# A selective scan's last D product moved over B's PSUM tile, and Gabor groups taken in pairs

## The chip, the cores and the metric

The kernel runs on one core of one Trainium2 chip. The metric is the device time of one execution in microseconds. A core has five engines that run side by side, each through its own instructions in order: TensorE (PE, matrix products, weight loads listed apart as PEld), VectorE (DVE), ScalarE (ACT), GpSimd (POOL) and SyncE (SP, which here only issues DMAs). They wait for each other by semaphores.

## The reference

The input is 4 images of 64 channels and 128x128 pixels. Four layers follow each other:

```python
# layer 0: Mamba block, 16 states, over all 65,536 pixels as one sequence
# layer 1: Gabor transform, two small block-diagonal products, softshrink, inverse
# layer 2: two 3x3 convolutions with batch norm, a channel gate, residual
# layer 3: two 3x3 convolutions; LayerNorm; Mamba block, 64 states, per image;
#          LayerNorm; feed-forward with a 3x3 depthwise convolution
def step(h, t):                      # the scan of both Mamba blocks, 128 inner channels
    h = h * exp(delta_t * A) + (delta_t * x_t) * B_t
    y_t = h @ C_t                    # y = ys + x * D;  y = y * silu(z)
```

In layer 1 each image is seen as a 128x128 grid with 64 channels. `R1`, an FFT over 32x32 blocks, two products with w1 and w2, a softshrink, an FFT back and a last product with the window give `I`, which is added to the image.

## The kernel before

**The scan (`_Mamba.run`, used by layers 0 and 3).** Time is cut into chunks of 1,024 pixels, 64 chunks a layer. Four of the states by 32 of the 128 channels fill the 128 partitions, so a *group* of four states takes four *steps* (j = 0 to 3, one for each quarter of the channels). Layer 0 has 4 groups a chunk, layer 3 has 16. A step has four parts:

- ACT computes `da` = exp(A·delta) into one of four buffers (L562);
- the input `bx` = delta·x·B is put into PSUM (below);
- DVE scans over the 1,024 columns (L599), from `da` and `bx`, into one of eight slots of `ring`;
- POOL multiplies the slot by C (L602), and PE later adds the states up into `y` (L419), which has one PSUM tile. The sums of a group are issued in the second and third step after its last; the first thing put into a chunk's `y` is x·D (L416), in the last step of its first group.

Groups come in two kinds, in a fixed order: "DADA" in layer 0, "DADAADAADADAADAA" in layer 3. In an *A* group ACT multiplies delta·x with B in transposed form (`bxT`, L393, 28 small instructions a group, and one block on POOL, L397), and PE transposes it into a PSUM tile for each step (L500, 8 transposes). In a *D* group PE spreads B over the partitions into one PSUM tile (L506), once for the group, and DVE multiplies it with a replicated copy of delta·x (`du`, one tile for each j, loaded by SP's DMAs) into a second PSUM tile (L593), for each step again into the same one.

PSUM has room for two `bx` tiles, which are taken in turn. So the transposes of the first A step after a D group take B's tile, and have to wait for the last product, which reads B.

The instructions of a step are written out in one order and each engine keeps it (`_Pin`): in step i come the `da` three steps ahead, bxT copies at a pace worked out from what is owed, the transposes for step i+1 (`produced(i + 1)`), the product of a D step, the scan, POOL's product, at most one entry of the list `owed` (y's first sums and the groups' sums), and at last pieces of the next and the last chunk's remaining work (`beside`): projections, convolution, normalisation, delta, all through one further PSUM tile `pm`. In layer 3 `budget` says how many pieces a step may issue: 2, 2, 2, 1 in the steps of a D group, none in A. In layer 0 it is 12 everywhere. The gating product `yg` = y·silu(z) (L625) is a DVE instruction in the last step of a chunk's first group, ahead of that step's product.

**The Gabor stage (`layer1`).** For each of 4 images and each of 4 groups of 16 channels PE runs a chain: fa (L1047, the image's columns, 16 products of 256 columns, copied by DVE to `Z`), fb (L1058, copied by ACT to `O`), w1 (L1071), w2 (L1078; DVE adds the bias and clamps, POOL subtracts the clamp: the softshrink, L1079 to L1082), ga (L1089, copied by ACT to `V`) and lt (L1100: for each of 32 rows two products of 64 columns, which DVE adds to the image, L1107). All six share four PSUM tiles. Each group waits for the one before it.

Of the kernel before, what the change touches and what calls it, by code (L numbers as in the profile page):

```python
# [10 lines left out]
F32 = mybir.dt.float32  # L11
AF = mybir.ActivationFunctionType
ALU = mybir.AluOpType
# [4 lines left out]
P = 128  # L18
B, C, HH, WW = 4, 64, 128, 128
HW = HH * WW  # L20
TC = 1024
NH = TC // 512
DI = 128
NUM, SIZE = 4, 32
NQ, DD = 4, 32
ND = DI // DD
# [5 lines left out]
G = 16  # L32
# [135 lines left out]
class _Mamba:  # L168
# [19 lines left out]
    def __init__(self, ctx, tc, K, nst, w, kinds, bufs, slots={}):  # L188
# [5 lines left out]
        self.dram = ctx.enter_context(tc.tile_pool(name="md", bufs=2, space=DRAM))  # L194
        self.bp = ctx.enter_context(tc.tile_pool(name="mb", bufs=1, space=PSUM))
        self.misc = ctx.enter_context(tc.tile_pool(name="mm", bufs=1, space=PSUM))

# [229 lines left out]
    def run(self, chunks, ahead, behind, leads, budget):  # L427
# [23 lines left out]
        reps = [(k, c, j) for c in chunks for k in ("dl", "du") for j in range(ND)]  # L451
        das, bxs = {}, {}
        nexp = nmul = nC = 0
# [37 lines left out]
        def produced(i):  # L491

            if i == n:
                return
            v, j = its[i]
            if v["kind"] == "A" or i == v["at"]:
                bx = bxs[i] = self.bp.tile([P, TC], F32, name="bx", tag="bx", bufs=2)
            if v["kind"] == "A":
                for k in range(NB):
                    nc.tensor.transpose(  # L500
                        bx[:, P * k : P * (k + 1)], v["bxT"][:, k, :, :, j].rearrange("p q e -> p (q e)"), self.K.eye
                    )
            elif i == v["at"]:
                v["B"] = bx
                for k in _COLS:
                    nc.tensor.matmul(bx[:, k], self.spread[v["g"]], v["c"]["xc"][:, k], start=True, stop=True)  # L506
# [25 lines left out]
        at = -1  # L532
# [5 lines left out]
        for i, (u, j) in enumerate(its):  # L538
# [46 lines left out]
            if full and full[0] <= i:  # L585
                started(behind(full[1], self.gated(full[1])), i)
                full = None
            produced(i + 1)
            if u["kind"] == "D":
                if i == u["at"]:  # L590
                    u["bx"] = self.bp.tile([P, TC], F32, name="bx", tag="bx", bufs=2)
                bxs[i] = u["bx"]
                nc.vector.tensor_mul(bxs[i], u["c"]["du"][j], u["B"])  # L593

# [4 lines left out]
            nc.vector.tensor_tensor_scan(  # L599
                hs, das.pop(i), bxs.pop(i), 0.0 if u["c"].get("reset") else st, ALU.mult, ALU.add  # L600
            )
            nc.gpsimd.tensor_mul(hc, hs, u["cb"])  # L602
            if j == ND - 1:
                nc.gpsimd.tensor_copy(self.state[:, :, u["g"]], self.ring[:, slot - j : slot + 1, GAP + TC - 1])
            u["hc"].append(hc)
            if i == u["last"]:
                owed += [(i, u, None)] * (u["g"] == 0) + [(i + 2, u, h) for h in range(NH)]
            while owed and not full and (owed[0][0] <= i or i + 1 == n):
# [362 lines left out]
def layer1(ctx, tc, K, w, x1, x2):  # L971
# [60 lines left out]
    MU = P // G  # L1032
    for b in range(B):
        X = xp.tile([P, HH, C], F32, name="X1", tag="X1")
        nc.sync.dma_start(X, x1[b].rearrange("c (h r w) -> (c h) r w", h=2, w=C))
        for g in range(NG):
            ch = slice(g * G, (g + 1) * G)

            def ps():
                return pa.tile([P, 1024], F32, name="p1", tag="p1")  # L1040


            Z = wp.tile([P, 2, P, G], F32, name="Z", tag="Z", bufs=2)
            for c0 in range(0, G, 4):
                p = ps().rearrange("p (c i m) -> p c i m", c=4, i=2)
                for c in range(4):
                    nc.tensor.matmul(  # L1047
                        p[:, c], X[:, :, g * G + c0 + c], fa.rearrange("p i m k -> p (i m k)"), start=True, stop=True
                    )
                nc.vector.tensor_copy(Z[:, :, :, c0 : c0 + 4].rearrange("p i m c -> p c i m"), p)  # L1050

# [22 lines left out]
            for k0 in range(0, G, 8):  # L1074
# [6 lines left out]
                nc.vector.tensor_scalar(cl, xs[:, ks], -LAMBD, LAMBD, ALU.max, ALU.min)  # L1081
                nc.gpsimd.tensor_sub(xs[:, ks], xs[:, ks], cl)  # L1082

            V = wp.tile([P, 2, G, P], F32, name="V", tag="V", bufs=2)
            xr = xs.rearrange("p k (m c) -> p (k m) c", c=G)
            for c0 in range(0, G, 4):
                p = ps().rearrange("p (c i m) -> p c i m", c=4, i=2)
                for c in range(4):
                    nc.tensor.matmul(  # L1089
                        p[:, c], xr[:, :, c0 + c], ga.rearrange("p i m k -> p (i m k)"), start=True, stop=True  # L1090
                    )
                nc.scalar.copy(V[:, :, c0 : c0 + 4, :].rearrange("p i c m -> p c i m"), p)

            Vl = V.rearrange("p i c (y l) -> p i l y c", l=SIZE)
            Xl = X[:, :, ch].rearrange("p (y l) c -> p l y c", l=SIZE)
            for l0 in range(0, SIZE, 16):
                p = ps().rearrange("p (l y c) -> p l y c", l=16, y=NUM)
                for l in range(16):
                    for i in range(2):
# [6 lines left out]
                        )  # L1106
                nc.vector.tensor_add(Xl[:, l0 : l0 + 16], Xl[:, l0 : l0 + 16], p)  # L1107
        nc.sync.dma_start(x2[b].rearrange("c (h r w) -> (c h) r w", h=2, w=C), X)
# [175 lines left out]
def layer3_mamba(ctx, tc, K, w, t3, x3, s3, n3):  # L1284
# [78 lines left out]
    chunks = [{"at": (b, t0), "reset": t0 == 0} for b in range(B) for t0 in range(0, HW, TC)]  # L1363
    m.run(chunks, ahead, behind, (64, 36), [x for k in m.kinds for x in ([2, 2, 2, 1] if k == "D" else [0] * ND)])

# [280 lines left out]
```

## Time and profile before

| what | value |
|---|---|
| median of 3 runs (lowest, highest) | 19,391.08 us (19,358.28, 19,392.66) |
| the profiled execution | 19,395.58 us, span 19,393.5 us |
| mean granted PE clock | 0.876 |
| DVE busy | 15,837.4 us (82%) |
| PE busy | 15,226.3 us (79%) |
| ACT busy | 14,924.4 us (77%) |
| POOL busy | 14,204.5 us (73%) |
| first and last scan of layer 0 | 68.3 and 3,663.0 us |
| first and last scan of layer 3 | 6,229.6 and 18,427.1 us |

In a line of the profile stand the line of the kernel, the engine, the operation, the tiles (written <- read), the shape and the count; then busy time, the mean of one in ns, the engine's idle time just before such instructions, and who ended it. A line of a timeline has the start, the length, the engine, the line, the operation and the count of equal instructions merged into it; idle time before it and its releaser stand in brackets. Lengths of neighbours can overlap. A matmul in fp32 shows as two records, a transpose as one.

### The profile page before, as it was taken

The page shows a single profiled execution, that of the slowest core. Times are in us where ns is not written, and L with a number is a line of the kernel's source. Part 1 is how long each engine was busy: PE and PEld are TensorE (multiplying, and loading weights), DVE is VectorE, ACT ScalarE, POOL GpSimd, SP SyncE. Part 2 cuts the span into 40 slices and gives each one's busy share as a digit, 9 for nine tenths or more (in the row PEclk, how much of TensorE's full clock was granted, in tenths as well). Part 3 has the DMA queues.
Part 4 walks back from the last instruction along what each step waited for, and adds up shares of the span by engine and source line. Part 5 has one row for each costly group of instructions (what it writes and reads, how often), then busy time and mean ns, then how long its engine had stood idle before and what let it go on. Part 6 is the DMA issues. An engine that isn't in the chain of part 4 may idle for free. (4 is left out here: it accounts for less than half of the span.)

```text
span 19393.5 us, 238514 instructions
## 1 busy us (share of the span) xinstructions
PE 15226.3 (79%) x80186; PEld 7611.8 (39%) x80186; DVE 15837.4 (82%) x8739; ACT 14924.4 (77%) x30369; POOL 14204.5 (73%) x8094
## 2 busy tenths in 40 slices
PE   7777878778797777777777777777777777777799
PEld 3333333367434333333333333333333333333323
DVE  7888888722113999999999999999999999999977
ACT  7888888501223898989889988989898988888833
POOL 6888888600001989898989989998989989898900
PEclk8989889879898888888888888888888888888899
DMA  5555555300122323232323233232323232323222
GB/s 140 148 156 150 151 154 150 116 38 27 34 69 74 84 78 87 75 88 76 87 76 86 80 83 83 79 87 76 88 76 87 76 86 78 84 80 82 73 56 55
DMA packets 669522, 1722.88 MB, mean 89 GB/s; under 512 B 196784, under 2 KB 231936, under 8 KB 660864
## 3 DMA queue, kind: packets, MB, share of 16 engines
q1 hardware_dynamic: 668288, 1707.62, 32.5%
q8 instruction: 629, 10.31, 0.2%
q14 instruction: 605, 4.96, 0.1%
HBM read 1434.27 MB, written 272.63 MB: 88 GB/s over the span
## 5 line engine op out<-in xcount | busy, mean ns | idle before, releaser
L602 POOL TENSOR_TENSOR ring<-ring,cb 128x1024 f32<-128x1024 f32 x5120 | 12081.8, 2376 | 1642.8 <-DVE ring L599 1335.9
L599 DVE TENSOR_TENSOR_SCAN ring<-da,state,bx 128x1024 f32<-128x1024 f32 x4848 | 11144.0, 2336 | 962.5 <-PE bx L500 687.9
L562 ACT ACTIVATE da<-dl,A 128x1024 f32<-128x1024 f32 x5120 | 5868.1, 1146 | 1370.1 <-DVE ring L599 1353.7
L393 ACT ACTIVATE bxT<-duT,BT 128x128 f32<-128x128 f32 x21504 | 6757.3, 387 | 0.0
L500 PE MATMUL bx<-cst,bxT 128*128 128x128 f32 x24576 | 4455.8, 338 | 2837.7 <-DVE bx L593 2045.6
L500 PEld LDWEIGHTS bx<-cst,bxT 128*128 128x128 f32 x24576 | 3740.9, 214 | 4905.5 <-DVE bx L593 2064.0
L419 PE MATMUL y<-ring,cst 128*32 128x512 f32 x20480 | 3560.4, 658 | 335.2 <-POOL ring L602 334.7
L593 DVE TENSOR_TENSOR bx<-du,bx 128x1024 f32<-128x1024 f32 x2048 | 2515.1, 1228 | 338.1 <-PE bx L506 217.5
L419 PEld LDWEIGHTS y<-ring,cst 128*32 128x32 f32 x20480 | 531.5, 112 | 1741.5 <-POOL ring L602 864.5
L1151 PE MATMUL cv<-img,cw 64*64 64x512 f32 x9216 | 1008.9, 594 | 76.3 <-DMA img<-d_x 45.5
L506 PE MATMUL bx<-xc,spread 128*128 128x512 f32 x2048 | 1016.9, 619 | 1.4
L1082 POOL TENSOR_TENSOR xs<-xs,cl 128x1024 f32<-128x1024 f32 x32 | 74.9, 2340 | 1066.7 <-DVE cl L1081 1066.7
L1316 POOL MEMSET X<- 64x1 f32 x4 | 0.4, 91 | 1125.1 <-DMA cw<-in_l_conv_wT 1125.1
L397 POOL TENSOR_TENSOR bxT<-duT,BT 128x512 f32<-128x512 f32 x768 | 809.0, 1053 | 11.9 <-ACT duT L376 11.9
L1151 PEld LDWEIGHTS cv<-img,cw 64*64 64x64 f32 x9216 | 435.8, 134 | 647.3 <-issue 534.8
L599 DVE TENSOR_TENSOR_SCAN ring<-da,bx 128x1024 f32<-128x1024 f32 x272 | 609.2, 2276 | 71.1 <-PE bx L500 49.4
L1447 ACT ACTIVATE h<-ph,ff_fc_b 128x384 f32<-128x384 f32 (+1 forms) x384 | 200.8, 577 | 594.2 <-PE ph L1442 576.5
L1433 POOL MEMSET h<- 128x18 f32 x64 | 8.3, 131 | 876.1 <-PE pd L1521 443.9
L1521 PE MATMUL pd<-h,diag 64*64 64x512 f32 x4608 | 632.1, 603 | 0.7 <-issue 0.7
L506 PEld LDWEIGHTS bx<-xc,spread 128*128 128x128 f32 x2048 | 347.6, 189 | 687.4 <-issue 463.6
L1467 DVE SCALAR_TENSOR_TENSOR g<-h,dww,g 128x2048 f32<-128x2048 f32 x256 | 602.0, 2351 | 11.4 <-DVE g L1467 0.5
L1065 ACT COPY O<-p 128x1024 f32<-128x1024 f32 x32 | 32.4, 1012 | 690.9 <-PE p L1058 690.9
(321 smaller groups left out, 13274.4 us busy)
## 6 DMA issues: line engine op xcount, KB each, us to landing
cb<-c SPq DMA_DIRECT2D x5120, 128.0 KB, 2.9
dl<-d SPq DMA_DIRECT2D x2048, 128.0 KB, 3.5
du<-d SPq DMA_DIRECT2D x2048, 128.0 KB, 3.1
d<-pos SPq DMA_DIRECT2D x128, 512.0 KB, 2.6
d<-u SPq DMA_DIRECT2D x128, 512.0 KB, 3.0
X<-d_t SPq DMA_DIRECT2D x124, 256.0 KB, 4.1
S<-in_x SPq DMA_DIRECT2D x120, 256.5 KB, 4.5
res<-in_x SPq DMA_DIRECT2D x128, 128.0 KB, 3.8
```

Of the source, the lines that this page charges most:

```text
L393: nc.scalar.activation(t[:, k, q].rearrange("p e j -> p (e j)"), c["duT"][:, k, :], AF.Copy, scale=c["BT"][:, k, n : n + 1])
L397: nc.gpsimd.tensor_mul(t[:, k].rearrange("p q e j -> p q (e j)"), c["duT"][:, k].unsqueeze(1).to_broadcast(shape), c["BT"][:, k, NQ * g : ...
L419: nc.tensor.matmul(c["y"][DD * j : DD * (j + 1), _COLS[h]], K.sel, hc[:, _COLS[h]], start=False, stop=u["g"] == self.ng - 1,)
L500: nc.tensor.transpose(bx[:, P * k : P * (k + 1)], v["bxT"][:, k, :, :, j].rearrange("p q e -> p (q e)"), self.K.eye)
L506: nc.tensor.matmul(bx[:, k], self.spread[v["g"]], v["c"]["xc"][:, k], start=True, stop=True)
L562: nc.scalar.activation(das[nexp], v["c"]["dl"][k], AF.Exp, scale=self.A[:, k, v["g"] : v["g"] + 1])
L593: nc.vector.tensor_mul(bxs[i], u["c"]["du"][j], u["B"])
L599: nc.vector.tensor_tensor_scan(hs, das.pop(i), bxs.pop(i), 0.0 if u["c"].get("reset") else st, ALU.mult, ALU.add)
L602: nc.gpsimd.tensor_mul(hc, hs, u["cb"])
L1151: nc.tensor.matmul(p[i][half[h]], W[half[i], k, :], src[half[i], at : at + 4, dx : dx + WW], start=k == 0, stop=k == 8,)
L1467: nc.vector.scalar_tensor_tensor(g1, tap, wk, g1, ALU.mult, ALU.add)
L1521: nc.tensor.matmul(pd[i][half[h]], diag[half[i], k, :], h0[half[i], r : r + 4, dx : dx + WW], start=k == 0, stop=k == 8,)
```

## The change

1. The two `bx` tiles are made once and addressed by number. B of a D group and the products of its steps 0, 1 and 2 stand as before, in two tiles. The product of step 3 is written over B, in place.
2. That product is issued in step 2, right behind step 2's own product, ahead of the scan of step 2. So DVE's order in a D group is product, scan, product, scan, product, product, scan, scan. The first A step after it takes the tile of the products, not B's.
3. Layer 3's budget in the last step of a D group is 0 instead of 1. In each chunk this moves one piece of the output projection from step 11 to step 20, and one piece of the next chunk's B from step 43 to step 52.
4. The entry of x·D in `owed` is made in the first step of the group instead of the last, with the same due step.
5. In the Gabor stage fa of the next group is issued ahead of ga of the present one, and lt runs once for two groups: 64 products of 128 columns instead of 128 of 64. `V` holds two groups, in one buffer instead of two. DVE's additions keep their number and size.

```diff
+        self.bx = [self.bp.tile([P, TC], F32, name=f"bx{k}") for k in range(2)]
...
-            if v["kind"] == "A" or i == v["at"]:
-                bx = bxs[i] = self.bp.tile([P, TC], F32, name="bx", tag="bx", bufs=2)
             if v["kind"] == "A":
+                at = tiles[i] = 1 - tiles.get(i - 1, 1)
+                bx = self.bx[at]
...
             elif i == v["at"]:
-                v["B"] = bx
+                at = 1 - tiles.get(i - 1, 1)
+                tiles.update({i + k: at if k == ND - 1 else 1 - at for k in range(ND)})
+                bx = v["B"] = self.bx[at]
...
+            bx = self.bx[tiles[i]]
             if u["kind"] == "D":
-                if i == u["at"]:
-                    u["bx"] = self.bp.tile([P, TC], F32, name="bx", tag="bx", bufs=2)
-                bxs[i] = u["bx"]
-                nc.vector.tensor_mul(bxs[i], u["c"]["du"][j], u["B"])
+                for k in {ND - 2: (ND - 2, ND - 1), ND - 1: ()}.get(j, (j,)):
+                    nc.vector.tensor_mul(self.bx[tiles[i - j + k]], u["c"]["du"][k], u["B"])
...
+            if i == u["at"] and u["g"] == 0:
+                owed.append((u["last"], u, None))
             if i == u["last"]:
-                owed += [(i, u, None)] * (u["g"] == 0) + [(i + 2, u, h) for h in range(NH)]
+                owed += [(i + 2, u, h) for h in range(NH)]
...
-    ... ([2, 2, 2, 1] if k == "D" else [0] * ND)])      # layer 3's budget
+    ... ([2, 2, 2, 0] if k == "D" else [0] * ND)])
...
+    def transformed(b, g):          # fa and Z, as before; loads the image where g is 0
+    Zn = transformed(0, 0)
     for b in range(B):
         for g in range(NG):
+            Z = Zn                  # then fb, w1, w2 and the softshrink, as before
...
-            V = wp.tile([P, 2, G, P], F32, name="V", tag="V", bufs=2)
+            if (b, g) != (B - 1, NG - 1):
+                Zn = transformed(*divmod(b * NG + g + 1, NG))
+            if g % 2 == 0:
+                V = wp.tile([P, 2, 2 * G, P], F32, name="V", tag="V")
+            v0 = g % 2 * G          # ga, copied to V[:, :, v0 + c0 : v0 + c0 + 4]
+            if g % 2 == 0:
+                continue
...
-            Xl = X[:, :, ch].rearrange("p (y l) c -> p l y c", l=SIZE)
-            for l0 in range(0, SIZE, 16):
-                p = ps().rearrange("p (l y c) -> p l y c", l=16, y=NUM)
-                for l in range(16):
+            Xl = X[:, :, (g - 1) * G : (g + 1) * G].rearrange("p (y l) c -> p l y c", l=SIZE)
+            for l0 in range(0, SIZE, 8):
+                p = ps().rearrange("p (l y c) -> p l y c", l=8, y=NUM)
+                for l in range(8):
```

## The prediction

> **What bounds the kernel now.** I read the busy times by stage first, then the page's costliest groups, then VectorE's (DVE's) timeline of one chunk, and last the timelines of TensorE (PE), ScalarE (ACT) and GpSimd (POOL) beside it. Times are in us. The columns of the stages are: stretch, its length, then busy time (instructions) of PE, PE's weight loads, DVE, ACT, POOL, then PE's granted clock, DMA share, GB/s.
>
> ```profile
> 0.00:3760.00 3760.00, 2955.29 (x14220) 1414.62 (x14224) 3172.96 (x1699) 3139.37 (x5790) 3081.19 (x1682) 0.90 0.56 149
> 4110.00:5010.00 900.00, 750.68 (x4736) 692.22 (x4736) 213.40 (x162) 132.79 (x128) 74.87 (x32) 0.91 0.07 31
> 6180.00:18420.00 12240.00, 9307.22 (x44215) 4612.26 (x44215) 11354.62 (x5756) 10967.22 (x23416) 10987.89 (x6205) 0.86 0.30 82
> ```
>
> Layer 3's scans (last line) hold 12,240 of 19,393.5. DVE is busy 93% there, but POOL and ACT are at 90%, so a stall removed on DVE need not come through. Layer 0 (first line) has no engine above 84%: it hops from engine to engine. In the Gabor stage (middle) PE alone works, 83%.
>
> Two groups from the page: the scan and POOL's product after it, one each per step.
>
> ```profile
> L602 POOL TENSOR_TENSOR ring<-ring,cb 128x1024 f32<-128x1024 f32 x5120 | 12081.8, 2376 | 1642.8 <-DVE ring L599 1335.9
> L599 DVE TENSOR_TENSOR_SCAN ring<-da,state,bx 128x1024 f32<-128x1024 f32 x4848 | 11144.0, 2336 | 962.5 <-PE bx L500 687.9
> ```
>
> POOL's 2.38 is more than the pitch of two scans (below), so in runs of A groups POOL falls behind; it catches up in D groups. DVE's largest idle is for PE's transposes (687.9). Where? DVE's timeline of one layer 3 chunk, whose steps I number 0 to 63 (step 2's product is at 10049.72, step 5's scan at 10062.04, step 13's at 10088.43):
>
> ```profile
> 10047.33 2.35 DVE L599 TENSOR_TENSOR_SCAN ring<-da,state,bx 128x1024 f32<-128x1024 f32 x1
> 10049.72 1.23 DVE L593 TENSOR_TENSOR bx<-du,bx 128x1024 f32<-128x1024 f32 x1
> 10051.05 2.35 DVE L599 TENSOR_TENSOR_SCAN ring<-da,state,bx 128x1024 f32<-128x1024 f32 x1
> 10053.31 1.20 DVE L625 TENSOR_TENSOR yg<-y,sz 128x1024 f32<-128x1024 f32 x1
> 10054.43 1.22 DVE L593 TENSOR_TENSOR bx<-du,bx 128x1024 f32<-128x1024 f32 x1
> 10055.75 4.58 DVE L599 TENSOR_TENSOR_SCAN ring<-da,state,bx 128x1024 f32<-128x1024 f32 x2
> 10062.04 6.82 DVE L599 TENSOR_TENSOR_SCAN ring<-da,state,bx 128x1024 f32<-128x1024 f32 x3 [1.71 <-PE bx L500]
> ...
> 10088.43 13.54 DVE L599 TENSOR_TENSOR_SCAN ring<-da,state,bx 128x1024 f32<-128x1024 f32 x6 [2.19 <-PE bx L500]
> ```
>
> The pitches: scan to scan 2.25 (6.82 for three is 2×2.25+2.32); scan to product 2.38; product to the scan that needs it 1.33; yg to a product that doesn't need it 1.12. So a D step costs 3.71. Stalls: steps 5 (1.71) and 13 (2.19). PE at those places:
>
> ```profile
> 10055.70 1.98 PE L500 MATMUL bx<-cst,bxT 128*128 128x128 f32 x8 [5.66 <-DVE bx L593]
> 10057.61 3.17 PE L416 MATMUL y<-xc,dD 128*32 128x512 f32 x16
> 10060.71 2.19 PE L500 MATMUL bx<-cst,bxT 128*128 128x128 f32 x16
> ...
> 10083.34 1.97 PE L282 MATMUL pm<-tr,cst 128*64 128x512 f32 x2
> 10085.10 1.91 PE L282 MATMUL pm<-yg,woT 128*64 128x512 f32 x2
> ```
>
> After group 1 PE waits 5.66 for the last product, does step 4's transposes, then 3.1 of D·x sums, and only then step 5's transposes. After group 2 a piece of the projection (3.6) stands between steps 12 and 13: the "1" in the budget.
>
> ACT's timeline shows what is behind step 13: it never idles from 10076.43 to 10104.2, and the last copies of step 16's bxT end at 10093.05, just where step 16's transposes start (10093.07).
>
> ```profile
> 10091.33 1.14 ACT L562 ACTIVATE da<-dl,A 128x1024 f32<-128x1024 f32 x1
> 10092.37 0.68 ACT L393 ACTIVATE bxT<-duT,BT 128x128 f32<-128x128 f32 x2
> ```
>
> Gabor, one group on PE:
>
> ```profile
> 4175.44 9.04 PE L1058 MATMUL p<-fb,Z 128*128 128x128 f32 x64 [1.96 <-DVE Z L1050]
> 4187.75 3.73 PE L1078 MATMUL p<-w,O 128*128 128x128 f32 x32
> 4197.47 9.95 PE L1089 MATMUL p<-ga,xs 128*128 128x256 f32 x32 [5.98 <-POOL xs L1082]
> 4208.52 14.54 PE L1100 MATMUL p<-V,lt 128*128 128x64 f32 x128 [1.10 <-ACT V L1092]
> ```
>
> **What the skill says.** The Trainium skill, Perfetto Trace Analysis, "Optimizing Scalar/DVE Operations": half of an instruction's fixed latency, the write acknowledgement, overlaps the next instruction. The trace agrees: scans of 2.35 stand 2.25 apart. VectorE: DVE Perf Modes, "The DRAIN you can't avoid": a same-engine read-after-write needs a semaphore or an instruction in between, and the semaphore is free; here it isn't: 1.33 dependent against 1.12 independent. TensorE: Matmul & The Clock Gate, "Back-to-back issue gap": spacing is set by weight load and matmul together. The trace agrees: 14.54/128 = 0.114 a record at 64 columns, 3.73/32 = 0.117 at 128. Same page, "What's actually happening": PE runs at half rate after an idle window of some 3.4; here eight transposes take 1.98 after 5.66 idle and 1.23 otherwise.
>
> **Gabor.** Removed: half of the 1,024 lt products; at the 128-column rate a pair of groups takes 64×0.233 = 14.9 in place of 2×14.36 (pitch): 13.8. Moved: the next group's fa products (7.34 on PE) and four Z copies (7.15 on DVE) go ahead of ga. They fill the 5.98 wait for POOL; Z is then early, and the 1.96 wait goes too. On DVE the Z copies queue behind the second clamp, which waits 1.41 for POOL; fa's four PSUM tiles are free by then (relu and xs are out of them), and ga's first tile follows one Z copy. The input load keeps its place on SP's queue. One 1.10 wait for V goes per pair. V has one buffer of double size; its readers end a whole group earlier, no cost. Per pair 13.8+2×5.98+2×1.96+1.10 = 30.8, times 8 = 246. With fewer gaps PE stays warm: fb 9.04 was 7.41 in groups where it ran fast (4121.54 to 4128.95), ga 9.95 could come to fa's 7.34; both fully would add 65. I take a third: **270**. Floor: the strided 128-column operand at fb's slow rate (0.28), 64×0.05×8 = 26 less than 246: 220. Top 310.
>
> **D groups on DVE.** Two products back to back were never run. I price product to product and product to an independent scan at yg's 1.12 (bounds: 1.0 and the dependent 1.33). Scan 1 to scan 3 was 3.71+3.71 = 7.43; now 2.38+1.12+1.12+2.25 = 6.87: 0.56. With 1.33 twice, 0.14. I take 0.54. The first D group of a chunk needs du3 one scan earlier, and scan 2 queues behind it; du's DMA waits were 53.5 in 3 times in all, so it is covered.
>
> **Group 1 (step 5).** Step 4's transposes now wait for scan 2 to end, not for a product two places later. From the end of scan 1: scan 2 ends 0.91 later, but the transposes follow at 0.06 in place of 2.31, then 1.98, D·x 3.1 (yg, which frees y, ends at 1.1: covered), step 5's transposes 1.23 and 0.11 to the scan. Scan 5 starts 6.44 after scan 2's end where it was 8.63; less 0.91: **1.28** a chunk. The two edits to the list of owed sums give the same order: nothing.
>
> **Group 2 (step 13).** The projection piece goes to step 20, behind the next B, where PE then waits over 5 before step 24: free there. DVE could win 2.29 (mean over chunks) + 0.54. But ACT's work from scan 9's end to the last copy for step 16 is 16.6, back to back; step 16's scan follows two transposes later, at about 17.2. Before it started at 18.64. So only **1.4** comes through; scan 16 becomes the new stall.
>
> **Other four D groups of layer 3.** 4×0.54 = **2.16**. But the last two scans now come 2.25 apart, so POOL enters the A run 0.13 later, and ACT (2.9 of work a D step) some 0.7 later; ACT's da is 4 or more ahead, so that is covered, POOL's delay reaches PE's sums in about three places: −0.45. Transposes after D: 0.06+1.98+0.11 = 2.15, just the pitch: no stall, no room. The second moved piece (B, step 43 to 52) stood in a stall of 0.03: nothing.
>
> Layer 3: 64×(1.28+1.4+2.16−0.45) = **280**. Bounds: 130 if the pair gives 0.14 and ACT holds longer; 400 if ACT costs nothing.
>
> **Layer 0.** Its budget stays. From step 4's transposes a chain runs over PE to the sz piece, ACT (waits 2.83 for it, then is full until the duT copy), PE, the conv piece, step 13. Moving its head by 1.28 moves all: 64×1.28 = **80**. Group 2's 0.54 is lost, since step 12's transposes wait for PE behind duT, not for DVE. Bounds 0 and 110.
>
> Sum 270+280+80 = 630, from the profiled span 19,393.5: 18,763. The profiled run was 19,395.6 and the median of three 19,391, so the two agree and I say **18,765**.
>
> **Rivals.** (1) *The stalls come through whole*: ACT's order gives no stall at step 16, PE warm in Gabor: 310+400+100 = 810, 18,585. For: DVE is the busiest engine. Against: ACT's 16.6. (2) *Other engines take it*: POOL's and ACT's 90% eat the D groups' gain; Gabor 240, groups 1 in both layers 110 remain: 350, 19,040. (3) *Slower*: step A0's transposes miss. Their tile is freed by scan 2 on paper; were they held until scan 3 ends (a wait put on the pair, or on B's tile), each of 512 D groups stalls 2.2: +1,130, net 500 slower, 19,890. It decides from 630/512 = 1.2 a group. Against: steps inside A runs already live on the same two-tile rhythm with 2.25. (4) *The pair is not independent* (1.33 twice): 0.4×(64×4) = 100 and some 40 elsewhere less, 18,900; inside the range.
>
> **How the numbers follow.** Forecast (with 4) 0.66, rival 1 0.12, rival 2 0.18, rival 3 0.03, no change 0.01 (the Gabor part alone is 1.1%). The forecast's own range is 18,640 to 18,900. With most of rivals 1 and 2 in, the range is 18,600 to 19,040. A measurement of this kernel tells 0.2% from nothing; faster 0.96, same 0.01, slower 0.03.
>
> **What would show it.** Gabor stage near 630 from 900, lt half as many at about 0.117 a record, no wait for POOL before ga. DVE: product, product, scan, scan at 1.12, 1.12, 2.25. Step 5's stall near 0.9, step 13's gone, a new one near 1.3 at step 16, released by PE behind ACT. Wrong if the first transposes after D stall each time, or if lt's records grow with the columns.

## The result, and the profile after

The kernel after takes 18,911.63 us (median of 4 runs, 18,908.64 to 18,916.54) where the kernel before takes 19,391.87 (median of 4): a ratio of 0.9757, 95% interval 0.974 to 0.9774. The profiled execution took 18,913.85 us, its span is 18,912.0, 481.5 less than before. I had said 18,765, within 18,600 to 19,040; the narrower range that I gave for the forecast itself, 18,640 to 18,900, it misses by 12.

By stage, from the starts of the first and last scans and the first and last instruction of the Gabor stage:

| stage | before | after | difference | my step |
|---|---|---|---|---|
| layer 0, first to last scan | 3,594.6 | 3,505.4 | -89.2 | -80 |
| Gabor, first fa to last addition | 896.6 | 707.2 | -189.4 | -270 |
| layer 3, first to last scan | 12,197.6 | 11,994.8 | -202.8 | -280 |
| all else | 2,704.7 | 2,704.6 | -0.1 | 0 |

The busy times by stage (same columns as before: stretch, length, PE, its weight loads, DVE, ACT, POOL, PE's granted clock, DMA share, GB/s), for the kernel after:

```profile
0.00:3670.00 3670.00, 2927.78 (x14176) 1410.24 (x14180) 3125.84 (x1698) 3145.87 (x5790) 3062.25 (x1682) 0.90 0.57 152
4025.00:4735.00 710.00, 689.18 (x3712) 639.98 (x3712) 210.68 (x162) 132.79 (x128) 75.85 (x32) 0.98 0.09 39
5950.00:17950.00 12000.00, 9140.82 (x44194) 4597.74 (x44194) 11277.13 (x5758) 10894.53 (x23399) 10983.96 (x6203) 0.86 0.31 83
```

In the Gabor stage PE went from 83% busy to 97%, and still the stage takes 707: its work itself did not shrink as I had reckoned. In layer 3 DVE's share went from 93 to 94% only, and POOL's and ACT's are 91 to 92%.

The page's groups of the scans and of the y sums:

```profile
L603 DVE TENSOR_TENSOR_SCAN ring<-da,state,bx 128x1024 f32<-128x1024 f32 x4848 | 11107.5, 2334 | 818.7 <-PE bx L501 613.0
...
L420 PE MATMUL y<-ring,cst 128*32 128x512 f32 x20480 | 3540.9, 650 | 431.8 <-POOL ring L606 428.7
```

DVE's idle time before scans fell by 144 only, and PE's wait for POOL before the y sums, 428.7 here, was 334.7. Where the stalls stand, in DVE's timeline of one chunk of layer 3 (step 1's scan is at 9896.71):

```profile
9899.09 2.36 DVE L597 TENSOR_TENSOR bx<-du,bx 128x1024 f32<-128x1024 f32 x2
9901.36 2.34 DVE L603 TENSOR_TENSOR_SCAN ring<-da,state,bx 128x1024 f32<-128x1024 f32 x1
9903.61 1.20 DVE L631 TENSOR_TENSOR yg<-y,sz 128x1024 f32<-128x1024 f32 x1
9904.73 4.58 DVE L603 TENSOR_TENSOR_SCAN ring<-da,state,bx 128x1024 f32<-128x1024 f32 x2
9910.63 6.82 DVE L603 TENSOR_TENSOR_SCAN ring<-da,state,bx 128x1024 f32<-128x1024 f32 x3 [1.33 <-PE bx L501]
...
9927.29 13.53 DVE L603 TENSOR_TENSOR_SCAN ring<-da,state,bx 128x1024 f32<-128x1024 f32 x6
9942.34 6.84 DVE L603 TENSOR_TENSOR_SCAN ring<-da,state,bx 128x1024 f32<-128x1024 f32 x3 [1.53 <-PE bx L501]
```

The pair is there nearly as I priced it: two products in 2.27 from the first's start to the next scan's start. Between the last two scans of this group stands `yg`; in the other D groups they are 2.25 apart. Step 5 (the line with 1.33) still stalls. Step 13 no longer does (six scans in 13.53). A new stall of 1.53 stands at step 16, where I had put one of about 1.3. PE's and ACT's timelines of the same chunk say why:

```profile
9903.75 1.98 PE L501 MATMUL bx<-cst,bxT 128*128 128x128 f32 x8 [4.33 <-DVE ring L603]
9905.67 3.64 PE L417 MATMUL y<-xc,dD 128*32 128x512 f32 x16
9909.24 2.25 PE L501 MATMUL bx<-cst,bxT 128*128 128x128 f32 x16
...
9941.70 1.47 PE L501 MATMUL bx<-cst,bxT 128*128 128x128 f32 x10 [1.82 <-ACT bxT L394]
```

```profile
9940.97 0.68 ACT L394 ACTIVATE bxT<-duT,BT 128x128 f32<-128x128 f32 x2
```

Step 4's transposes start 0.05 after scan 2 ends (9903.70), so rival 3 did not happen; D·x stands behind them as before. At step 16 PE waits 1.82 for ACT's last copies.

The Gabor stage, the end of one pair of groups and the next group on PE:

```profile
4125.81 7.32 PE L1073 MATMUL p<-fb,Z 128*128 128x128 f32 x64
...
4139.98 7.31 PE L1054 MATMUL p<-fa,X 128*128 128x256 f32 x32
4147.13 7.26 PE L1108 MATMUL p<-ga,xs 128*128 128x256 f32 x32
...
4183.88 28.40 PE L1121 MATMUL p<-V,lt 128*128 128x128 f32 x128 [1.10 <-ACT V L1111]
```

No gap before ga or fb, and both at their quick rate. But lt for two groups takes 28.40: 0.222 us a record, where I had put 0.117 (a product in fp32 is two records). Two groups before took 2 x 14.54 = 29.08.

### The profile page after: what moved, and what is told of

It is laid out like the page before. It is cut to its first block, busy times and chain, and to the rows that moved or that the text cites. A ratio compares the mean times of both kernels' runs of the same rounds, so it can differ in the third digit from the quotient of the medians.

```text
span 18912.0 us, 236473 instructions
## 1 busy us (share of the span) xinstructions
PE 14994.4 (79%) x79162; PEld 7682.6 (41%) x79162; DVE 15705.1 (83%) x8739; ACT 14875.0 (79%) x30369; POOL 14184.7 (75%) x8094
## 5 line engine op out<-in xcount | busy, mean ns | idle before, releaser
L501 PE MATMUL bx<-cst,bxT 128*128 128x128 f32 x24576 | 4533.6, 342 | 2609.5 <-DVE ring L603 2512.6
L501 PEld LDWEIGHTS bx<-cst,bxT 128*128 128x128 f32 x24576 | 3781.1, 214 | 4575.2 <-DVE ring L603 3647.4
L420 PE MATMUL y<-ring,cst 128*32 128x512 f32 x20480 | 3540.9, 650 | 431.8 <-POOL ring L606 428.7
L597 DVE TENSOR_TENSOR bx<-du,bx 128x1024 f32<-128x1024 f32 x2048 | 2467.0, 1227 | 318.5 <-PE bx L510 206.6
L1172 PEld LDWEIGHTS cv<-img,cw 64*64 64x64 f32 x9216 | 567.8, 134 | 514.0 <-issue 403.3
L283 PE MATMUL pm<-S,cw 128*128 128x512 f32 x1024 | 543.6, 667 | 14.3 <-ACT sz L315 13.0
```

The source lines that it names most:

```text
L420: nc.tensor.matmul(c["y"][DD * j : DD * (j + 1), _COLS[h]], K.sel, hc[:, _COLS[h]], start=False, stop=u["g"] == self.ng - 1,)
L501: nc.tensor.transpose(bx[:, P * k : P * (k + 1)], v["bxT"][:, k, :, :, j].rearrange("p q e -> p (q e)"), self.K.eye)
L597: nc.vector.tensor_mul(self.bx[tiles[i - j + k]], u["c"]["du"][k], u["B"])
L1172: nc.tensor.matmul(p[i][half[h]], W[half[i], k, :], src[half[i], at : at + 4, dx : dx + WW], start=k == 0, stop=k == 8,)
```

## The experiments

Times are medians; ratios are to the kernel before, run on the same chip beside them. Stages are first to last scan and first fa to last addition, in the profiled execution.

| kernel | us | ratio, 95% interval | Gabor | layer 3 |
|---|---|---|---|---|
| after | 18,911.6 | 0.9757 (0.974 to 0.9774) | 707.2 | 11,994.8 |
| Gabor part alone | 19,197.7 | 0.9898 (0.9881 to 0.9914) | 706.5 | 12,207.6 |
| after, V's channel inner | 18,813.9 | 0.97 (0.9686 to 0.9715) | 609.8 | 11,994.7 |
| before, V's channel inner | 19,594.2 | 1.0107 (1.0092 to 1.0122) | 1,120.7 | 12,170.3 |
| after, budget back | 18,875.8 | 0.9732 (0.9717 to 0.9746) | 704.0 | 11,958.0 |
| after, pair undone | 18,751.7 | 0.9668 (0.9654 to 0.9682) | 706.6 | 11,842.8 |
| after, D·x split | 18,906.2 | 0.9757 (0.9742 to 0.9771) | 706.7 | 11,991.0 |
| after, copies earlier | 18,758.7 | 0.9681 (0.9666 to 0.9695) | 704.1 | 11,845.2 |
| after, sums later | 19,164.2 | 0.989 (0.9875 to 0.9904) | 704.0 | 12,247.3 |
| pair undone, V inner, sums later | 18,839.7 | 0.9732 (0.9713 to 0.9751) | 609.0 | 12,011.5 |
| pair, V, copies, D·x, sums together | 18,934.7 | 0.9767 (0.975 to 0.9783) | 609.3 | 12,114.7 |
| pair undone, V, copies, sums together | 19,090.6 | 0.9845 (0.983 to 0.9859) | 608.8 | 12,285.0 |
| pair in four groups, V, copies | 18,550.4 | 0.9569 (0.9556 to 0.9582) | 609.4 | 11,733.8 |

Layer 0 is 3,503.9 to 3,505.4 in every kernel that has the change in the scan, pair or no pair, and 3,576.9 to 3,594.6 in those that have not; layer 3 is 12,170.3 to 12,207.6 in the latter. So the same scan code repeats there to 18 us in layer 0 and 37 in layer 3 only; with the change, the two kernels that differ in V's layout alone agree to 0.5 and 0.1.

For the scan, the means over layer 3's chunks of the time from the scan before to a step's scan (a D pitch was 3.71, an A pitch is 2.25), and of POOL's lag, from the end of a step's scan to the start of POOL's product of it (the lag without the layer's first chunk):

| | before | after | budget back | pair undone | copies earlier | pair in four |
|---|---|---|---|---|---|---|
| step 5 | 4.00 | 3.35 | 2.96 | 2.31 | 3.20 | 2.25 |
| step 13 | 4.53 | 2.25 | 2.69 | 2.24 | 2.24 | 2.24 |
| step 16 | 2.25 | 3.66 | 3.39 | 3.13 | 2.25 | 2.27 |
| step 19 | 2.86 | 3.05 | 3.06 | 2.40 | 2.39 | 2.27 |
| step 39 | 3.56 | 3.36 | 3.03 | 3.01 | 3.24 | 3.24 |
| step 47 | 2.82 | 3.23 | 2.60 | 3.41 | 3.25 | 3.02 |
| step 51 | 2.39 | 3.38 | 3.70 | 2.32 | 3.37 | 2.45 |
| all 64 | 190.65 | 187.48 | 186.91 | 185.10 | 185.14 | 183.40 |
| POOL's lag at step 3 | 0.37 | 1.69 | | 0.39 | 1.69 | 0.39 |
| POOL's lag at step 43 | 1.10 | 2.55 | | 1.23 | 2.55 | 1.23 |

**The Gabor part alone.** The functions of the scan and layer 3's budget stay as before.

> The kernel before with the Gabor part of the change alone. If the Gabor part is worth what the two traces show of its stage (896.6 to 707.2 us from the first fa product to the last addition), it gives 189 us: 19,203 us, with 0.206 us a record in the lt products. My prediction gave this part 270 us: 19,122. If part of the 189 came from the layers (an earlier or later hand-over, or a clock that is granted after a different load), the stage is not at 707 here: more than 10 us away from it.

Measured: 19,197.65, the stage 706.5. The part is worth what the traces show, whichever scan stands beside it, and not my 270.

**V with the channel innermost.** The same edit in two kernels: in the one after (two groups, runs of 32 channels) and in the one before (one group, runs of 16).

```diff
-                V = wp.tile([P, 2, 2 * G, P], F32, name="V", tag="V")
+                V = wp.tile([P, 2, P, 2 * G], F32, name="V", tag="V")
...
-                nc.scalar.copy(V[:, :, v0 + c0 : v0 + c0 + 4, :].rearrange("p i c m -> p c i m"), p)
+                nc.scalar.copy(V[:, :, :, v0 + c0 : v0 + c0 + 4].rearrange("p i m c -> p c i m"), p)
...
-            Vl = V.rearrange("p i c (y l) -> p i l y c", l=SIZE)
+            Vl = V.rearrange("p i (y l) c -> p i l y c", l=SIZE)
```

> The kernel after, with V laid out with the channel innermost, so that the 128 columns of an lt product lie in runs of 32 neighbours where they were 512 bytes apart; ScalarE's copies into V then write 128 bytes apart. Theory 1, the distance of the operand's columns costs the time: a record goes from 0.206 us to the 0.117 that other products of 128 columns take (w2 3.73 for 32), a pair of groups from 26.4 to about 15, the stage from 707 to about 616, the kernel from 18,912 to about 18,820. Theory 2, 128 columns against a 128 x 128 weight cost 0.206 in this stage whatever their layout: the kernel stays within 15 us of 18,912, or is slower if the copies of V take longer (1.10 us waited for now; 64 copies).

Measured: 18,813.94; the stage 609.8. One pair's lt on PE:

```profile
4166.94 16.18 PE L1121 MATMUL p<-V,lt 128*128 128x128 f32 x128 [1.96 <-ACT V L1111]
```

16.18 in place of 28.40 for the same products: theory 1. Six of the eight pairs take this at a granted clock of 0.89; the first and the last take 14.56 at 1.00, which is 0.114 us a record, the rate that I had reckoned with. So the distance of 512 bytes between neighbouring columns of the moving operand (the one that streams past the loaded weight, here V) set the record's time: 28.40/128/128 = 1.73 ns a column. The records with 64 such columns fit the same rate, 14.54/128/64 = 1.77. The copies of V pay for the new layout: they take 1.92 us in place of 1.01, and the wait for V is 1.96. The Trainium skill's SBUF — State Buffer, "Door 1: The DMA port swizzle", says that SBUF is read in lines of 16 bytes and that an access that crosses to a new line pays; the measurement, 28.40 against 14.56 at full clock, agrees in direction.

> The kernel before with V laid out with the channel innermost and nothing else. It tells what the 0.114 us a record of the lt products with 64 columns was. Theory 1, the operand's distance of 512 bytes: a record falls to between 0.06 and 0.08, 16 groups x 128 records x 0.035 to 0.054 = 70 to 110 us faster than before: 19,290 to 19,320, and merging two groups would have been worth little by itself. Theory 2, at 64 columns a record costs its weight load, as my prediction had it: it stays at 0.114 and the time within 15 us of 19,390.

Measured: 19,594.23, and 1,120.7 for the stage: 224 slower. Neither theory had that. PE is busy 420.3 us with lt in place of 232.6, and 150.1 with fa in place of 119.1. The first lt stretch in the busy times and in PE's timeline:

```profile
4149.00:4174.00 25.00, 25.00 (x129) 25.00 (x129) 1.22 (x1) 0.00 (x0) 0.00 (x0) 0.55 0.00 1
```

```profile
4148.84 25.33 PE L1100 MATMUL p<-V,lt 128*128 128x64 f32 x128 [1.96 <-ACT V L1092]
```

The granted clock is 0.51 to 0.55 in all sixteen lt stretches, though PE's records follow each other without a gap; in the kernel before it was 1.00 in them. So this run does not give the cost of a 64-column record at full clock (at about half clock it is 0.197 to 0.213), and whether 0.114 was also a weight load stays open: a record with 128 near columns takes 0.114 too. What the two runs show is that the layout loses by itself and pays beside the rest of the Gabor part. Whether it is the merge or the earlier fa that makes the difference was not tried.

**Layer 3's budget back to [2, 2, 2, 1].**

> The kernel after with layer 3's budget [2, 2, 2, 1] as before: the projection piece is back between steps 12 and 13. Theory, ScalarE holds step 16: the stall of about 2.25 us at step 13 returns and that of 1.41 at step 16 vanishes, since ScalarE gets the time that VectorE loses: 64 x 0.85 = 54 us slower, 18,966. Rival A, step 16 waits for something else, made by the pair: both stalls stand, 64 x 2.25 = 144 slower, 19,056. Rival B, step 13's stall is not this piece's: step 13 stays at 2.25 and the time within 10 us of 18,912.

Measured: 18,875.84 (18,870.78 to 18,883.15), below all four runs of the kernel after. Layer 3 is at 11,958.0, 37 us below the kernel after and below the run with V's channel inner, which stood beside it: the moved pieces cost that much. Step 13 is at 2.69, not 4.5. So my reading, that the projection piece made its stall, was the smaller part of it: step 12's transposes began 1.32 after scan 10's end then and begin 0.05 after it now, and with that most of the piece has its place. What fell is the theory that the budget moved the stall. The 37 us come from steps 5, 16, 39 and 47, each quicker by 0.27 to 0.63, against 13, 45 and 51; PE's granted clock in layer 3 is 0.89 there and 0.86 in the kernel after. Why was not tried.

**The pair undone.** The last D product stays over B's tile but goes back to its own step.

```diff
-                for k in {ND - 2: (ND - 2, ND - 1), ND - 1: ()}.get(j, (j,)):
+                for k in (j,):
```

> The kernel after with the last D product at its old place in the order, between the last two scans, but still over B's tile. Scan 1 to scan 3 of a D group returns from 6.91 to 7.43 us. Theory, the pair is worth 0.52 only where nothing else sets the pace: in layer 3 four groups lose 0.52 each (2.1 a chunk), in group 2 step 16's stall shrinks by what the pair loses (0), in group 1 step 5's stall of 0.9 goes and 0.4 is won, because step 4's transposes need only scan 2; in layer 0 nothing is lost, because PE's chain starts at scan 2's end: 64 x 1.7 = 110 slower, 19,020. Rival, the 0.52 counts whole in all 512 groups: 266 slower, 19,178. Rival 2, most of the gain of layers 0 and 3 is the order (product ahead of the scan) and not the tile: over 290 slower, 19,200, with step 5's stall back at 1.7.

Measured: 18,751.68, 160 us *faster* than with the pair. All three expectations had it slower. Layer 3 loses 152 us of its 12,000 by the pair; the rest of the change, the tile above all, had won 355. In the D groups the pair does save 0.38 each (scan 1 to scan 3 is 7.28 without it, 6.90 with it; the rest of the old 7.43 is the tile's). But steps 5, 16, 19, 39 and 51 lose 1.04, 0.53, 0.65, 0.35 and 1.06. They have no common cause.

Step 5 waits for PE's D·x: with the pair scan 3 starts 1.33 sooner after scan 2, and D·x is no longer covered. Step 51 waits for POOL. POOL's timeline at steps 42 and 43, with the pair:

```profile
10024.87 2.38 POOL L606 TENSOR_TENSOR ring<-ring,cb 128x1024 f32<-128x1024 f32 x1 [2.57 <-DVE ring L603]
10027.18 2.38 POOL L357 TENSOR_TENSOR u<-pos,xc 128x1024 f32<-128x1024 f32 x1
10029.52 2.38 POOL L606 TENSOR_TENSOR ring<-ring,cb 128x1024 f32<-128x1024 f32 x1
```

and without it (the chunk before):

```profile
9782.00 2.36 POOL L606 TENSOR_TENSOR ring<-ring,cb 128x1024 f32<-128x1024 f32 x1 [1.36 <-ACT pos L352]
9784.32 2.36 POOL L357 TENSOR_TENSOR u<-pos,xc 128x1024 f32<-128x1024 f32 x1
9786.65 2.36 POOL L606 TENSOR_TENSOR ring<-ring,cb 128x1024 f32<-128x1024 f32 x1
```

The first line of each is step 42's product. With the pair, scan 2 of a group ends 0.93 later (4.65 in place of 3.71 after scan 1), so POOL sits idle 2.57 there. From then on it is busy without a break, because another product of 2.38 (`u`) is queued between those of the last two scans, and it starts this stretch 0.93 later against a DVE that is 0.38 earlier: 1.31, just what its lag at steps 3 and 43 grew by. Step 3 has `S` in that place. As POOL's 2.38 is over the scans' 2.25, the lag lasts: at step 47, the last of the next group, it is 3.02 in place of 1.54. PE's sums of that group wait for this product, and step 51's transposes stand behind them. PE, then DVE, in the chunk with the pair:

```profile
10040.57 1.06 PE L420 MATMUL y<-ring,cst 128*32 128x512 f32 x6
10042.42 1.04 PE L420 MATMUL y<-ring,cst 128*32 128x512 f32 x2 [0.79 <-POOL ring L606]
```

```profile
10044.73 2.35 DVE L603 TENSOR_TENSOR_SCAN ring<-da,state,bx 128x1024 f32<-128x1024 f32 x1 [0.89 <-PE bx L501]
```

In the mean over the chunks PE idles 0.90 for POOL there, and 0.04 without the pair. Steps 16, 19 and 39 are taken up with the next runs.

**Three edits that each aim at one stall.** D·x in two halves:

```diff
-                owed.append((u["last"], u, None))
+                owed += [(u["last"] + k, u, -1 - k) for k in range(NH)]     # one 512-column half each
```

> The kernel after with the D*x sums in two halves, one at step 3 and one at step 4 (16 products of 0.2 us between step 4's and step 5's transposes become 8). Theory, step 5's stall (3.35 against 2.25) is PE's D*x sums: it goes, 64 x 1.1 = 70 us in layer 3, nothing in layer 0 if its chain to step 13 is the same length as before, and 55 there if that chain starts at step 5: 18,840 or 18,785. Rival, the time is taken again at the next wait for POOL (step 19), since POOL loses the time in which it caught up: within 25 us of 18,912.

Measured: 18,906.24, no difference. Step 5 goes from 3.35 to 2.29 while POOL's lag at step 3 stays at 1.69, so its stall is PE's D·x and not POOL; but steps 19, 27, 8 and 63 grow by 0.53, 0.27, 0.26 and 0.19. That is the rival's time, but not its reason. POOL's lag at step 5 goes from 0.92 to 2.00, so that stall was time in which POOL caught up; by step 12 the lag is as before (0.43 against 0.42), so it accounts for step 8 at most.

At step 19 it is PE's granted clock. PE in two neighbouring chunks of the kernel after, each time the transposes of step 18, the sums of a group and the transposes of step 19:

```profile
9757.78 1.23 PE L501 MATMUL bx<-cst,bxT 128*128 128x128 f32 x8 [1.01 <-DVE ring L603]
9758.94 1.08 PE L420 MATMUL y<-ring,cst 128*32 128x512 f32 x8
9760.02 1.23 PE L501 MATMUL bx<-cst,bxT 128*128 128x128 f32 x8
...
9944.75 1.98 PE L501 MATMUL bx<-cst,bxT 128*128 128x128 f32 x8 [1.58 <-DVE ring L603]
9946.66 1.94 PE L420 MATMUL y<-ring,cst 128*32 128x512 f32 x8
9948.52 1.98 PE L501 MATMUL bx<-cst,bxT 128*128 128x128 f32 x8
```

The work is the same, and both times it begins 0.06 after scan 16's end, but the clock is 1.00 in the first and 0.50 in the second, and scan 19 starts 2.24 and 3.77 after scan 18. Over the chunks of the kernel after, step 19 takes 2.24 in the 28 where this stretch has a clock over 0.95 and 3.72 in the 34 where it is under 0.6; POOL's product is done before the sums begin in both, by 1.0 and 1.8 in the mean. With D·x in halves the clock is under 0.6 in 56 of the 63 chunks. What decides the clock there was not tried.

Five of ACT's copies brought into steps 4 to 7:

```diff
             credit += slope * (upto[i + 1] - upto[i])
+            credit += {4: 1.0, 5: 2.0, 6: 1.0, 7: 1.0}.get(i % per, 0.0) if per == 64 else 0.0
```

> The kernel after with five more of ScalarE's bxT copies brought into steps 4 to 7 of each chunk of layer 3 (5 x 0.345 = 1.7 us less for ScalarE between steps 8 and 16). Theory, step 16's stall of 1.41 us is ScalarE's last copy for its group: it falls to 0.2 or less. If nothing takes it again, 64 x 1.2 = 77 us faster, 18,835; if POOL's lag takes it at step 19 (lag 0.38 now), about 64 x 0.5 = 32 faster, 18,880. Rival, step 16 waits for something else: the stall stands at 1.4 and the time within 20 us of 18,912.

Measured: 18,758.69, twice the gain. Step 16 is at 2.25, so its stall was ACT's copies. Step 19 falls with it (3.05 to 2.39), where I had thought POOL might take some back; POOL's lag there is 1.80 now, and 0.38 before, and it does not stop the scan. PE's clock in the stretch before step 19 is over 0.95 in 49 of the 63 chunks now, and under 0.6 in none. How the stall at 16 bears on that clock was not tried by itself.

The y sums of layer 3 one step later:

```diff
-                owed += [(i + 2, u, h) for h in range(NH)]
+                owed += [(i + 2 + (self.ng > 4 and u["g"] < self.ng - 1), u, h) for h in range(NH)]
```

> The kernel after with the y sums of all groups but the last of a chunk in layer 3 asked for one step later (three and four steps after a group's last scan, not two and three). Theory, the pair's gain was lost because TensorE's sums wait for POOL's product of the group's last step and the next transposes stand behind them: POOL starts that product 1.5 to 3.4 us after the scan's end at steps 19, 27, 39, 47, 51, 59 and 63, and the steps there are 0.3 to 1.1 us over 2.25, 5.1 us a chunk. One step (2.25) more covers most of it: 3 to 5 us a chunk, 190 to 320 us faster, 18,590 to 18,720. Rival, POOL's own throughput is the bound and the wait only moves, to the scans that need its place in the ring: under 60 us faster, over 18,850.

Measured: 19,164.23, 253 *slower*. Steps 19, 27, 39, 47, 51, 59 and 63 are all at 2.23 to 2.24, so their stalls are indeed transposes that stand behind sums. That the sums wait for POOL holds at step 51, though, in part at 47 (POOL's product ends 0.8 after they begin), and not in general: in the kernel after, POOL's product is done 0.8 to 2.0 before the sums begin at steps 19, 27, 39, 59 and 63 (means), and PE does not wait for it. What makes those stretches long is the clock, 0.57 to 0.83 in the mean there and 0.98 at step 51. With the sums gone from there, step 19's transposes find room at a mean clock of 0.58 too. But steps 12, 24, 36, 44 and 56 are at 3.83 to 4.10: the scan five steps after a group takes the group's slot of the ring, and now waits for the sums (468 us in all, a wait that was not there):

```profile
L603 DVE TENSOR_TENSOR_SCAN ring<-da,state,bx 128x1024 f32<-128x1024 f32 x3840 | 8781.4, 2332 | 688.8 <-PE y L420 468.2 <-POOL bxT L398 70.1 <-ACT da L566 27.8
```

The wait moved to the ring, as the rival had it, but it is PE's late sums that are waited for there, not POOL's throughput.

**Candidates.** The first joins V's layout, the pair undone and the later sums:

> A candidate: the kernel after with the last D product back in its old place in the order (over B's tile), V with the channel innermost, and the sums one step later. The first two alone would give 18,752 - 97 = 18,655. Theory: the sums' waits for POOL cost about 0.2 + 0.2 + 0.75 + 1.15 + 0.25 = 2.5 us a chunk there (steps 19, 27, 39, 47, 59), and the later sums take up to that off: 18,500 to 18,560. Rival, POOL's throughput: 18,620 to 18,655.

Measured: 18,839.66: 185 over the 18,655 that the first two alone would give by their own runs; the later sums lose here too. The next two ask for both sums of a group in one step, three after its last scan, where an A group follows:

```diff
-                owed += [(i + 2, u, h) for h in range(NH)]
+                u["both"] = self.ng > 4 and self.kinds[u["g"] + 1 :][:1] == "A"
+                owed += [(i + 2 + u["both"], u, h) for h in range(NH)]
...
-                if i + 1 < n:
+                if i + 1 < n and not (v["both"] and h == 0):
                     break
```

> The kernel after, pair kept, with V's channel innermost (97 us measured), five copies earlier in steps 4 to 7 (153 measured), the D*x sums in two halves, and the two y sums of a group that an A group follows both asked for three steps after its last scan (where the later sums of the other run were late for the ring, after D groups, they keep their old places). Theory, the waits for POOL at steps 19, 27, 39, 47, 51, 59 and 63 are worth 4.0 us a chunk beside the copies, and step 5's stall 0.95: 18,662 - 256 - 60 = 18,350 at best, 18,430 if a third comes back elsewhere. Rival, POOL (169 us busy of 187 a chunk) is the bound and the ring takes the gain: 18,600 or more.

> The same without the pair (the last D product over B's tile, in its old place in the order) and without the split of the D*x sums. From 18,752 less V's 97, step 16's stall of 0.88 (56) and the waits at steps 19, 27, 39, 47 and 59 of 2.6 (166 at best): 18,433 at best, 18,500 if a third comes back. Against the run with the pair: if the pair's loss was the waits that the other edits take away, that run is 50 to 100 us faster than this; if the pair costs by itself, this is faster. Rival, POOL is the bound: 18,600 or more, and the two within 40 us of each other.

Measured: 18,934.72 and 19,090.56, far behind. The stalls at steps 19, 27, 39, 47, 51, 59 and 63 are gone again (2.23 to 2.25), but step 16, which the copies had freed, is back at 2.96 and 3.40, and others stand at the first product of D groups (step 52 from 4.20 to 6.01 with the pair, step 20 from 4.05 to 5.55). PE's and then DVE's timeline at step 52 with the pair:

```profile
9786.99 3.64 PE L421 MATMUL y<-ring,cst 128*32 128x512 f32 x16
9790.56 2.17 PE L511 MATMUL bx<-xc,spread 128*128 128x512 f32 x4
```

```profile
9792.77 1.23 DVE L599 TENSOR_TENSOR bx<-du,bx 128x1024 f32<-128x1024 f32 x1 [3.25 <-PE bx L511]
```

Both sums together take 3.64 here, at a granted clock of 0.50 (2.99 at 0.68 in the mean), and B waits behind them: over a step's 2.25. The expectation had priced the wait taken away, not the place taken, nor the clock. The one that keeps the pair is the quicker of the two (12,114.7 against 12,285.0 in layer 3), so the pair need not cost beside other edits (this kernel has D·x in halves as well, which alone did nothing).

**The pair in four groups.** This tests where the pair costs: it is taken back in the two groups of layer 3 where `S` and `u` stand between the last two products on POOL; V's layout and the earlier copies, each measured alone, are in as well.

```diff
-                for k in {ND - 2: (ND - 2, ND - 1), ND - 1: ()}.get(j, (j,)):
+                late = {} if self.ng > 4 and u["g"] in (0, 10) else {ND - 2: (ND - 2, ND - 1), ND - 1: ()}
+                for k in late.get(j, (j,)):
```

> The kernel after with V's channel innermost, the five copies earlier, and the pair taken back in two of layer 3's six D groups, those at steps 0 to 3 and 40 to 43, where POOL has another product of 2.37 us (S, u) between those of the last two scans; the other four groups and layer 0 keep it. To be compared with the run that has the five copies alone: its layer 3 is 11,845 us from first to last scan. Theory, the pair makes scan 2 end 0.93 later and scan 3 begin 0.38 earlier, so that a POOL that is busy from then on starts its queue 0.93 later against a VectorE that is 0.38 earlier, 1.31 in all (its lag after the scan at step 3 is 1.69 with the pair and 0.39 without, at step 43 2.55 and 1.23): without it there the lags are back at 0.4 and 1.25, step 5 falls from 3.20 to about 2.3 and step 51 from 3.37 to about 2.3, for 2 x 0.38 us a chunk; with 0.3 at step 52 that is 64 x 1.5 = 96 us, layer 3 at 11,750, the kernel at 18,759 - 97 - 96 = 18,566. Rival, the pair costs in all groups alike or its loss is at other steps: steps 5 and 51 gain less than 0.5, layer 3 within 30 us of 11,845, the kernel at 18,630 to 18,700.

Measured: 18,550.39 (18,546.56 to 18,556.18), layer 3 11,733.8, 111 less than with the copies alone. The lags are at 0.39 and 1.23, step 5 falls by 0.95, step 51 by 0.92, and some steps that the two groups do not reach stand as they were (36, 39, 53 to 58), while 15 and 59 grow by 0.31 and 0.39. So most of the pair's loss, 111 here where 152 was lost without the copies, lies in these two groups. But the expectation gives POOL's lag as the reason for both, and it is shown for step 51 only, where PE's idle time for POOL falls from 0.93 to 0.10; step 5 is D·x again, which scan 3 covers when it comes 1.33 later. The same kernel with the pair undone in all six groups was not run, so that the pair pays in the four others is not shown.

This kernel beats the one before by 4.3% and the one after by 1.9%.

## Why the prediction was right in sign, and where its working was wrong

The time fell into the range, 147 us above the value. The range was wide, since it took in most of two rivals, and the sum held less well than its total: of its terms, some came true, and one was credited with what another did.

- **Layer 0, 80.** Measured 89 (71 against the Gabor part alone). The reason given (PE's chain starts at scan 2's end, the pair's own gain is lost) agrees: without the pair layer 0 takes 3,504.7, the same.
- **Gabor, 270.** Measured 189. The waits for POOL, Z and V fell from 144.6 to 16.8, 128 where I had 136. PE stayed quick throughout: fb and ga took 52 less, of 65 possible, where I took 24. The term that failed is "at the 128-column rate a pair of groups takes 14.9": it took 28.4, and lt saved 5.5 in place of 110. I had taken 3.73/32 from a product whose columns lie side by side; lt's lie 512 bytes apart. 14.54/128 = 0.114 looked like the price of the weight load and fits 64 distant columns as well. My floor of 220 allowed for a slow clock, not for this, and "wrong if lt's records grow with the columns" was the sentence to have priced.
- **The pair, 0.56 a group.** Measured 0.52 in its place, 6.90 from scan 1 to scan 3, with product to product at 1.14 and product to a scan that does not need it at 1.13, near the 1.12 priced. A dependent scan still follows its product 1.33 later. Rival 4 is out, though the time came within 12 of its 18,900. But the *worth* of the pair is -152 us in layer 3, where the sum had 4 x 0.54 less 0.45 a chunk for it, 109.
- **The failed step in the scan** is this credit. "POOL enters the A run 0.13 later" holds in the four groups where nothing stands between POOL's last two products (lag 0.27 against 0.17 at step 23), and is 1.31 in the other two; at step 51 that costs 1.06 a chunk, 68 us. I had looked at scan 3, which comes earlier, and not at scan 2, which comes 0.93 later and holds up all that is queued behind its product. Step 5 costs about as much, by D·x, and steps 19 and 39 are slow with PE's clock, which the sum had only in the Gabor stage and at step 4. Its "1.98 after 5.66 idle and 1.23 otherwise" for eight transposes was too simple: in the kernel before, those of step 18 take 1.92 in the mean after 1.02 idle.
- **Group 1, 1.28.** Steps 2 to 5 gained 1.06, and 1.69 without the pair: with scan 3 1.33 earlier than without it, step 5 has too little to cover PE's D·x.
- **Group 2, 1.4.** Steps 10 to 19 gained 1.07, with the stall at step 16 where and as large (1.41 in the mean) as said, and for the reason said, ACT. But I credited the budget with step 13's stall; the tile takes most of it, and the budget edit, beside the pair, loses 37.
- **Other four D groups, 1.71 after POOL's share.** Steps 20 to 63 gained 1.26 of layer 3's 3.17 a chunk.
- **Rivals.** 3 did not happen: step 4's transposes start 0.05 after scan 2. 2 said that POOL and ACT eat the pair's gain, and they do in part (steps 51 and 16); D·x and the clock were not in it.

That layer 3 missed by 77 only is luck in part: without the pair its gain is 355 where the sum had 171 in groups 1 and 2, and the pair took 152 where the sum gave it 109. So the scan's gain is that of the tile (with the smaller edits beside it, which were not all run apart): first transposes of an A run that need not wait for the last product. The order, the part of the edit that shortens DVE's own work, gives back 152 of 355.

## What to carry to other kernels

When an engine's instructions are reordered to save time on it, look at the instruction that comes *later* by it, and at what is queued behind its consumer on the next engine: with POOL busy 92% in layer 3, a scan that ends 0.93 later cost 1.06 at step 51 where the group's order had won 0.38. A stall is not worth its own length: with the four engines at 75% and more, D·x in halves took one of 1.06 away and won nothing, five ACT copies moved took one of 1.41 and won 2.34 a chunk, and two ways to ask for the sums later, in four kernels, removed the stalls at the steps aimed at and were slower than without them. Before a wait is put down to an engine, look at the clock of the stretch: step 19 took 2.24 at full clock and 3.72 at half, in the same kernel. And a record's time from a product with another layout of its operands is no price for a merged one.

## What was not expected of the hardware

- A record of an fp32 product whose moving operand has its columns 512 bytes apart costs 1.73 to 1.77 ns a column at full clock; in runs of 32 neighbours, 14.56/128/128 = 0.89. ACT's copy of 1,024 columns takes 1.92 us when it writes 128 bytes apart and 1.01 in runs of 128 neighbours.
- PE was granted half its clock while its records followed each other without a gap (0.51 to 0.55 over stretches of 25 to 27 us), with 64 columns in runs of 16 against a 128 x 128 weight; with the same 64 columns 512 bytes apart it had 1.00. The Trainium skill, TensorE: Matmul & The Clock Gate, "What's actually happening", ties the clock to how busy the array has been; no run here tells what counts as busy in this stretch.
- Eight transposes, eight records of sums and eight transposes took 3.47 us in the mean at full clock and 5.71 at half; in the kernel after the same place in a chunk had the one in 28 chunks and the other in 34.
- A product that does not write the tile that the scan before it reads starts 2.26 after that scan's start, one that does 2.38: 0.12 of the 0.14 that the tile alone saves in a D group.
